# Folded cross attention: folding by pieces, outputs by two batches, norm by four tiles, the last batch by halves

## The chip, the cores and the metric

One core of a Trainium2 chip runs the whole network in one launch. The metric is the device time in microseconds. A core has a matrix engine, TensorE (PE in the profile, its weight loads PEld), a vector engine, VectorE (DVE), a scalar engine, ScalarE (ACT), a general one, GpSimd (POOL), and SyncE (SP), which here only issues transfers. Each runs its own queue of instructions in order. TensorE writes to PSUM, which has eight banks of 128 x 512 float32.

## The reference

Four layers, each a cross attention, a mixer and a mixture of experts, all in float32, over x of 16 batches x 64 tokens x 256. The change is in the cross attention of the second and the third layer (names L1_xattn and L2_xattn), both with this reference, on x after a layer norm without weights, and a context of 1024 tokens x 192 a batch:

```python
def _L2_xattn_ref(x, context, Wq, Wk, Wv, Wo, bo):
    HEADS = 8
    DIM_HEAD = 64
    SCALE = DIM_HEAD ** (-0.5)
    q = (x @ Wq).reshape(B, Nq, HEADS, DIM_HEAD)
    k = (context @ Wk).reshape(B, context.shape[1], HEADS, DIM_HEAD)
    v = (context @ Wv).reshape(B, context.shape[1], HEADS, DIM_HEAD)
    sim = jnp.einsum('bihd,bjhd->bhij', q, k) * SCALE
    attn = jax.nn.softmax(sim, axis=-1)
    out = jnp.einsum('bhij,bjhd->bihd', attn, v)
    return out.reshape(B, Nq, HEADS * DIM_HEAD) @ Wo + bo
...
x = x + _L2_xattn_ref(_layernorm(x, axis=-1), ctx_768, ...)
```

## The kernel before

`xattn_folded` never forms keys or values. It multiplies queries by Wk first ("folding": qw has 192 rows a head, so that scores are qw times the raw context), and applies Wv after the weighted sum of the context. x stands in SBUF as `X`, eight tiles of 128 tokens; `xn` is its norm and `xnT` the transposed norm.

- **Head of a stage.** `norm_T` (line 244) runs the layer norm of all eight tiles: statistics on DVE, the inverse root on POOL (`rsqrt`), the scaling on DVE, eight transposes of four tiles on PE into two banks, two copies; the second four tiles follow. Then `folded(0)`.
- **Folding.** For a group of G = 4 batches (256 tokens), `queries(g, m)` makes the queries of two heads (two matmuls to psq, a scaled copy to qT on ACT) and `fold(g, m)` multiplies them by Wk (four matmuls of 64 rows to two banks psqw, copies by DVE and ACT to qw). `folded` runs all four m in one go; in the main loop it stands ahead of the scores of the group's first batch.
- **Main loop.** A step is half a batch (four heads), 32 steps. In it PE makes the scores of the next step (`scores`: 64 matmuls into four banks pss, with the sums of the last step, psm, between), then the value products of the batch before: `values` (four matmuls of 512 columns on the first 128 context columns) in each half, and `others` (eight, on the other 64) in the second half. Steps with h = 0 are short, those with h = 1 long. DVE finds the maxima (`least`), ACT takes exponentials (`exps`), both scale by the inverse sums (`shares`), DVE transposes (`turn`). `keep` copies a finished batch out of banks o0 and o1 into oc.
- **Outputs.** Every G2 = 4 batches, one batch late, `output` multiplies oc by Wv (16 matmuls pso of 256 columns into two banks), copies them to oT by DVE and ACT, and multiplies two token tiles by Wo (psy), each added to X by DVE.
- **Banks.** `ps_s` has five banks (tag s: scores, psq, psqw, transposes), `ps_t` one (tag t: psm, pso, psy), `ps_o` two (o0, o1).
- **Beside it.** The second cross attention also computes the taps of the next mixer (`conv_taps`, steps 3 to 11: two pieces a step, each POOL, ACT, POOL, DVE in turn); the third takes the context's statistics (`ctx_sigma`, 16 DVE instructions and a root on POOL) in each long step. `add_row` adds the bias row to X on POOL.

After `set_order(True)` the order of PE is that of the code, by `mm` and `tr`, and so is that of DVE and ACT for calls through `dve` and `act` (`in_order` ties each instruction to the one before it on its engine). What is issued through `nc.vector` is placed by the scheduler. Line 188 is `mm`, 191 `tr`, 251 the transposes of `norm_T`, 72 every call through `dve` or `act`.

## Time and profile before

| what | time |
|---|---|
| median of 3 runs (3170.1 to 3172.38) | 3171.4 us |
| the profiled execution | 3170.8 us |
| its span, first to last instruction | 3168.8 us |
| PE busy in the span | 2940.9 us (93%) |
| DVE, ACT, POOL busy | 1960.3, 1348.4, 712.7 us |
| mean granted PE clock | 0.953 |

The second cross attention lies at about 748.7 to 1208.9 us of the span, the third at 1641.0 to 2104.0. In a profile line, "out<-in" are the program's names, "128*32 128x256 f32" the tile of the array and the moving operand, "x64" how many records are merged; a float32 matmul has two records. A bracket tells how long the engine was idle just before and whose end released it. Matmuls are pipelined, so a merged line's duration runs a little past the start of the next.

### The profile page before, as it was taken

What the parts mean: (1) busy time and instruction counts of PE and PEld (TensorE: products, weight loads), DVE (VectorE), ACT (ScalarE), POOL (GpSimd) and SP (SyncE); (2) the same over time, 40 slices, a digit from 0 to 9 for tenths busy, and PEclk for the clock granted to TensorE, in tenths of its full rate; (3) what the DMA queues carried; (4) which work ended last, traced back from release to release, by engine and by line L of the source; (5) the groups of instructions that cost most, each with busy time, mean ns of one, the idle gap of its engine ahead of it and who ended that gap; (6) DMA issues with size and microseconds to landing.
All of it is one profiled execution on the core that took longest, in us unless ns stands there. A gap on an engine that the chain in (4) does not pass through costs nothing.

```text
span 3168.8 us, 64106 instructions
## 1 busy us (share of the span) xinstructions
PE 2940.9 (93%) x26912; PEld 1772.9 (56%) x26912; DVE 1960.3 (62%) x4061; ACT 1348.4 (43%) x3035; POOL 712.7 (22%) x784
## 2 busy tenths in 40 slices
PE   7999999898899999979978999997999899998797
PEld 4666666665445544458854545434665455556676
DVE  6888886524666665971127676757884676765611
ACT  3555554312554541013324454438861255654211
POOL 1000002411110001014411000024771355541131
PEclk9999999999999999978988999998999999999889
DMA  2000000013223313017851222201111211210233
GB/s 74 32 32 32 28 22 15 14 37 105 61 78 92 98 45 82 21 65 270 294 162 53 70 71 73 59 21 39 41 54 37 64 57 63 70 44 14 94 108 122
DMA packets 73793, 223.00 MB, mean 70 GB/s; under 512 B 17457, under 2 KB 28580, under 8 KB 66594
## 3 DMA queue, kind: packets, MB, share of 16 engines
q1 hardware_dynamic: 45936, 113.99, 11.9%
q0 software_dynamic: 21840, 99.39, 9.4%
q10 hardware_dynamic: 5730, 5.53, 0.6%
q8 instruction: 212, 3.47, 0.5%
q14 instruction: 75, 0.61, 0.1%
HBM read 210.00 MB, written 12.66 MB: 70 GB/s over the span
## 4 chain that ended last, share of the span: by engine, by line
PE 79%; DVE 9%; issue 4%; ACT 4%; POOL 3%; DMA 1%; SPq 0%; ACTq 0%; POOLq 0%; DVEq 0%
PE pss L188 13%; PE o L188 12%; PE pu L188 6%; PE psp L188 5%; PE pkv L188 5%; PE pd L188 5%; PE py L188 4%; PE pst L191 4%; PE psc L188 3%; PE po L188 2%; DVE nm L72 2%; ACT pr L72 2%; PE pb L191 2%; PE psi L188 1%; PE psq L188 1%
## 5 line engine op out<-in xcount | busy, mean ns | idle before, releaser
L188 PE MATMUL pss<-cT,qw 128*32 128x256 f32 x8192 | 371.5, 387 | 23.0 <-ACT pr L72 23.0
L72 DVE TENSOR_REDUCE nm<-pss 128x2 f32<-128x512 f32 (+1 forms) x384 | 309.3, 861 | 86.3 <-PE pss L188 86.3
L188 PE MATMUL o<-pT,cx 128*64 128x512 f32 (+1 forms) x1024 | 355.4, 607 | 0.0
L72 ACT ACTIVATE pr<-pss,nmm 128x256 f32<-128x256 f32 x512 | 234.3, 483 | 164.8 <-DVE nmm L72 164.8
L188 PEld LDWEIGHTS pss<-cT,qw 128*32 128x32 f32 x8192 | 205.0, 110 | 173.0 <-ACT pr L72 33.1
L188 PEld LDWEIGHTS o<-pT,cx 128*64 128x64 f32 (+1 forms) x1024 | 127.8, 165 | 200.2 <-issue 187.8
L205 POOL TENSOR_SCALAR rs<-mv 128x8 f32<-128x8 f32 (+3 forms) x52 | 10.0, 193 | 877.1 <-DVE mv L221 444.4
L188 PE MATMUL pkv<-wx,cT 128*128 128x512 f32 (+1 forms) x512 | 193.3, 632 | 0.6 <-issue 0.6
L72 ACT ACTIVATE pr<-pr,sm 128x256 f32<-128x256 f32 x256 | 109.1, 497 | 184.2 <-DVE sm L72 184.2
L72 DVE TENSOR_SCALAR pr<-pr,sm 128x256 f32<-128x256 f32 (+1 forms) x384 | 170.6, 486 | 6.6
L72 DVE TENSOR_TENSOR_SCAN h<-dA,pb 128x512 f32<-128x512 f32 x128 | 154.5, 1217 | 15.8 <-PE pb L191 9.4
L1444 POOL TENSOR_TENSOR h<-h,cb 128x1024 f32<-128x1024 f32 x64 | 151.4, 2368 | 53.3 <-DVE h L72 51.0
L2304 DVE TENSOR_SCALAR y<-pd,row 128x256 f32<-128x256 f32 x39 | 18.9, 484 | 225.1 <-PE pd L188 175.7
L72 DVE STREAM_TRANSPOSE pT<-pr 128x1024 f32<-128x1024 f32 x128 | 151.8, 1224 | 2.2
L188 PE MATMUL pd<-wd,hT 128*128 128x256 f32 x656 | 149.3, 382 | 3.0 <-DVE hT L2492 1.4
L72 ACT ACTIVATE pr<-pss,nm 128x1024 f32<-128x1024 f32 x128 | 142.5, 1113 | 11.4 <-DVE nm L72 8.8
L191 PE MATMUL pst<-ident,pr 128*128 128x128 f32 x1024 | 140.6, 280 | 5.8 <-DVE sm L72 1.9
L72 ACT COPY pT<-pst 128x512 f32<-128x512 f32 x128 | 74.9, 585 | 163.8 <-PE pst L191 163.8
L191 PEld LDWEIGHTS pst<-ident,pr 128*128 128x128 f32 x1024 | 109.4, 141 | 61.5 <-ACT pT L72 26.5
L188 PEld LDWEIGHTS pd<-wd,hT 128*128 128x128 f32 x656 | 123.1, 190 | 31.4 <-DVE hT L2492 6.2
L1618 POOL TENSOR_TENSOR rnk<-rnk,mhalf 128x8 f32<-128x8 f32 (+1 forms) x84 | 130.0, 1548 | 7.0
L188 PE MATMUL py<-h,ident 128*128 128x512 f32 x256 | 130.7, 596 | 0.0
(525 smaller groups left out, 5700.2 us busy)
## 6 DMA issues: line engine op xcount, KB each, us to landing
cT<-in_ctxT SPq DMA_DIRECT2D x32, 768.0 KB, 4.4
cx<-in_ctxP SPq DMA_DIRECT2D x32, 768.0 KB, 4.3
cT<-in_ctxT SPq DMA_DIRECT2D x32, 512.0 KB, 4.3
cT<-in_ctxT SPq DMA_DIRECT2D x64, 256.0 KB, 6.1
offb<-d_off SPq DMA_DIRECT2D x16, 576.0 KB, 3.6
cb<-d_C SPq DMA_DIRECT2D x16, 512.0 KB, 3.8
wu<-in_L_ffn_w POOLq DMA_DIRECT2D x8, 1024.0 KB
wd<-in_L_ffn_w POOLq DMA_DIRECT2D x8, 1024.0 KB
```

The costliest lines, as they stand in the source:

```text
L72: ins = getattr(self.engine, op)(*args, **kwargs)
L188: self.in_order(self.nc.tensor.matmul(out, lhsT=lhsT, rhs=rhs, start=start, stop=stop))
L191: self.in_order(self.nc.tensor.transpose(out, in_, self.ident))
L205: nc.gpsimd.tensor_scalar(t[:p, :n], in_, scale, eps, ALU.mult, ALU.add)
L1444: nc.gpsimd.tensor_tensor(hs[i], hs[i], cbs[hf, g], ALU.mult)
L1618: nc.gpsimd.tensor_tensor(r, r, self.mhalf[:, : n * H], ALU.pow)
L2304: nc.vector.tensor_scalar(y[:, i, :], po[:, i * D : (i + 1) * D], weight[:, g + i : g + i + 1], None, ALU.mult)
```

## The change

Both stages change alike, as they are one function:

- `fold` is split: it makes one pair of heads, into a bank of ps_s and bank o1 (at the start, when nothing else uses them, also into o0 and t), and the new `folded` copies it. From group 1 on, the short steps hold one fold each and the long steps one `queries` each, so that a fold follows its queries by a step. qT is copied by DVE, not ACT. qw is now a tile for four heads, four buffers.
- G2 is 2: `heads` (16 matmuls of 128 columns into one bank t, one copy by ACT) runs in the short step of every second batch, `output` (one token tile) in the long step after it.
- The norm runs by four tiles, its instructions through `dve` and `act`: the first four ahead of the loop, the others in steps 1 (statistics), 2 (scaling) and 3 (transposes). An activation of one element with Exp stands ahead of all.
- Ahead of the loop all four queries of group 0 and the first of group 1 are made, then two folds, the scores of four heads, and then the other two folds.
- In the last step `values` of the batch before stands ahead of the sums; the last batch's products are made for columns 0 to 255 and then 256 to 511, with one `keep` after both.
- `add_row` is called in step 5 instead of step 2.

```diff
--- before.py
+++ after.py
@@ -522,7 +522,7 @@
-        G, G2 = 4, 4
+        G, G2 = 4, 2
         T, T2 = G * TQ, G2 * TQ
         with ExitStack() as es:
             one = es.enter_context(tc.tile_pool(name=f"{L}one", bufs=1))
@@ -534,42 +534,67 @@
 
-            self.norm_T(ps_s, "s")
+
+            stats = one.tile([P, NT, 6], F32, name="stats")
+            mv = one.tile([P, NT, 2], F32, name="mv")
+            rs = one.tile([P, NT], F32, name="rs")
             self.set_order(True)
-            qws, qTs, ctxs, cxs, pTs, outs, ocs = ({} for _ in range(7))
+
+            act.activation(self.small.tile([P, 1], F32, tag="scrap", name="scrap"), self.ones[:, 0:1], AF.Exp)
+            qws, qTs, ctxs, cxs, pTs, outs, ocs, oTs = ({} for _ in range(8))
 
             def bank(name):
                 return ps_s.tile([P, 512], F32, tag="s", name=name)
 
+            def norm(g):
+                ts = slice(4 * g, 4 * g + 4)
+                for t in range(4 * g, 4 * g + 4):
+                    dve.bn_stats(stats[:, t, :], self.X[:, t, :])
+                    dve.bn_aggr(mv[:, t, :], stats[:, t, :])
+                self.rsqrt(rs[:, ts], mv[:, ts, 1], 1.0, 1e-5, 4)
+
+            def normed(g):
+                for t in range(4 * g, 4 * g + 4):
+                    dve.tensor_scalar(
+                        self.xn[:, t, :], self.X[:, t, :], mv[:, t, 0:1], rs[:, t : t + 1], ALU.subtract, ALU.mult
+                    )
+
+            def norm_T(g):
+                for c, copy in enumerate((dve.tensor_copy, act.copy)):
+                    ps = bank("psT")
+                    for k in range(4):
+                        self.tr(ps[:, k * P : (k + 1) * P], self.xn[:, 4 * g + k, c * P : (c + 1) * P])
+                    copy(self.xnT[:, c, g * 512 : (g + 1) * 512], ps)
+
             def queries(g, m):
 
                 tok = slice(g * T, (g + 1) * T)
-                qT = qTs[m] = two.tile([P, T], F32, tag="qT", name="qT")
+                qT = qTs[g, m] = two.tile([P, T], F32, tag="qT", name="qT", bufs=5)
                 ps = bank("psq")
                 for k in range(2):
                     self.mm(ps[:, :T], wq[:, k, m * P : (m + 1) * P], self.xnT[:, k, tok], k == 0, k == 1)
-                act.mul(qT, ps[:, :T], float(DK**-0.5))
-
-            def fold(g, m):
-
-
-                if m == 0:
-                    qws[g] = two.tile([P, 2, G, H, TQ], F32, tag="qw", name="qw", bufs=1)
-                qT = qTs[m]
-                pss = [bank("psqw") for _ in range(2)]
+                dve.tensor_scalar(qT, ps[:, :T], float(DK**-0.5), None, ALU.mult)
+
+            def fold(g, m, other=False):
+
+                if m % 2 == 0:
+                    qws[g, m // 2] = two.tile([P, 2, G, 4, TQ], F32, tag="qw", name="qw", bufs=4)
+                qT = qTs[g, m]
+                if other:
+                    pss = [pool.tile([P, 512], F32, tag=n, name="psqw") for pool, n in ((ps_o, "o0"), (ps_t, "t"))]
+                else:
+                    pss = [bank("psqw"), ps_o.tile([P, 512], F32, tag="o1", name="psqw")]
                 for i in range(2):
                     for hh in range(2):
                         r = slice(hh * DK, (hh + 1) * DK)
                         self.mm(pss[hh][:, i * T : (i + 1) * T], wkT[r, m, i * P : (i + 1) * P], qT[r, :])
-                for hh, copy in enumerate((dve.tensor_copy, act.copy)):
-                    copy(qws[g][:, :, :, 2 * m + hh, :], pss[hh].rearrange("p (i b q) -> p i b q", i=2, q=TQ))
-
-            def folded(g):
-                queries(g, 0)
-                for m in range(4):
-                    if m < 3:
-                        queries(g, m + 1)
-                    fold(g, m)
+                return g, m, pss
+
+            def folded(g, m, pss):
+                for hh, copy in enumerate((act.copy, dve.tensor_copy)):
+                    copy(
+                        qws[g, m // 2][:, :, :, 2 * (m % 2) + hh, :], pss[hh].rearrange("p (i b q) -> p i b q", i=2, q=TQ)
+                    )
 
             def load(b):
 
@@ -592,14 +617,14 @@
                 if h == 0:
                     load(b)
                 c0, c1 = ctxs[b]
-                qw = qws[b // G]
+                qw = qws[b // G, h]
                 pss = [bank("pss") for _ in range(4)]
 
                 def score(k, u, i, rows, start, stop):
                     for qa in range(4):
                         self.mm(
                             pss[k][qa * 32 : (qa + 1) * 32, u * 256 : (u + 1) * 256],
-                            qw[rows, i, b % G, 4 * h + k, u * 32 : (u + 1) * 32],
+                            qw[rows, i, b % G, k, u * 32 : (u + 1) * 32],
                             (c0, c1)[i][rows, :, qa, :],
                             start,
                             stop,
@@ -666,18 +691,22 @@
                     pr.rearrange("p q (k y) -> p q k y", y=32),
                 )
 
-            def values(b, r):
-
-                if r == 0:
-                    outs[b] = [ps_o.tile([P, 512], F32, tag=n, name=n) for n in ("o0", "o1")]
-                for j in range(4 * r, 4 * r + 4):
-                    self.mm(outs[b][0], cxs[b][:, j, 0:P], pTs[b][:, j], j == 0, j == NKC - 1)
-
-            def others(b):
-
+            def values(b, js, cols=slice(0, 512)):
+
+                if js[0] == 0 and cols.start == 0:
+                    outs[b] = [ps_o.tile([P, 512], F32, tag="o0", name="o0"), None]
+                for j in js:
+                    pT = pTs[b][:, j].rearrange("p q x -> p (q x)")
+                    self.mm(outs[b][0][:, cols], cxs[b][:, j, 0:P], pT[:, cols], j == 0, j == NKC - 1)
+
+            def others(b, cols=slice(0, 512)):
+
+                if cols.start == 0:
+                    outs[b][1] = ps_o.tile([P, 512], F32, tag="o1", name="o1")
                 for j in range(NKC):
                     rows = slice((j % 2) * 64, (j % 2 + 1) * 64)
-                    self.mm(outs[b][1][rows, :], cxs[b][:, j, P:C], pTs[b][:, j], j < 2, j >= NKC - 2)
+                    pT = pTs[b][:, j].rearrange("p q x -> p (q x)")
+                    self.mm(outs[b][1][rows, cols], cxs[b][:, j, P:C], pT[:, cols], j < 2, j >= NKC - 2)
 
             def keep(b):
                 if b % G2 == 0:
@@ -686,43 +715,50 @@
                 for i, o in enumerate(outs[b]):
                     (dve.tensor_copy, act.copy)[i](ocs[b // G2][:, i, :, ts], o.rearrange("p (h q) -> p h q", q=TQ))
 
-            def output(g2):
+            def heads(g2):
+
                 oc = ocs[g2]
-                oT = one.tile([P, 4, T2], F32, tag="oT", name="oT")
-                for mp in range(2):
-                    ps = (ps_t, ps_s)[mp].tile([P, 2, T2], F32, tag="ts"[mp], name="pso")
-                    for mi in range(2):
-                        for i in range(2):
-                            for hh in range(2):
-                                h = 4 * mp + 2 * mi + hh
-                                self.mm(
-                                    ps[hh * DK : (hh + 1) * DK, mi, :],
-                                    wv[:, i, h * DK : (h + 1) * DK],
-                                    oc[:, i, h, :],
-                                    i == 0,
-                                    i == 1,
-                                )
-                    (dve.tensor_copy, act.copy)[mp](oT[:, 2 * mp : 2 * mp + 2, :], ps)
-                for tt in range(T2 // P):
-                    t = g2 * T2 // P + tt
-                    ps = ps_t.tile([P, 512], F32, tag="t", name="psy")
-                    for m in range(4):
-                        self.mm(ps[:, :D], oT[:, m, tt * P : (tt + 1) * P], wo[:, m, :], m == 0, m == 3)
-                    dve.tensor_tensor(self.X[:, t, :], self.X[:, t, :], ps[:, :D], ALU.add)
-
-            folded(0)
+                oT = oTs[0] = one.tile([P, 4, T2], F32, tag="oT", name="oT")
+                ps = ps_t.tile([P, 4, T2], F32, tag="t", name="pso")
+                for m in range(4):
+                    for i in range(2):
+                        for hh in range(2):
+                            h = 2 * m + hh
+                            self.mm(
+                                ps[hh * DK : (hh + 1) * DK, m, :], wv[:, i, h * DK : (h + 1) * DK], oc[:, i, h, :], i == 0, i == 1
+                            )
+                act.copy(oT, ps)
+
+            def output(t):
+                ps = ps_t.tile([P, 512], F32, tag="t", name="psy")
+                for m in range(4):
+                    self.mm(ps[:, :D], oTs[0][:, m, :], wo[:, m, :], m == 0, m == 3)
+                dve.tensor_tensor(self.X[:, t, :], self.X[:, t, :], ps[:, :D], ALU.add)
+
+            norm(0)
+            normed(0)
+            norm_T(0)
+            for m in range(4):
+                queries(0, m)
+            queries(1, 0)
+            for m in range(2):
+                folded(*fold(0, m, m == 1))
             steps = [(b, h) for b in range(B) for h in range(2)]
             pss = scores(0, 0, None)
-            now = exps(pss, least(pss))
+            pieces = [fold(0, m, m == 3) for m in (2, 3)]
+            m = least(pss)
+            for x in pieces:
+                folded(*x)
+            now = exps(pss, m)
             st = {}
             for i, (b, h) in enumerate(steps):
                 ahead = steps[i + 1] if i + 1 < len(steps) else None
-                if ahead and ahead[0] % G == 0 and ahead[1] == 0:
-                    folded(ahead[0] // G)
+                g, at = (i + 1) // 8, (i + 1) % 8
                 prs, sm = now
                 if ahead:
                     pss = scores(*ahead, lambda: sums(st, sm))
                 else:
+                    values(b - 1, range(4, NKC))
                     sums(st, sm)
                 dve.reciprocal(sm, st["sum"][:, :8])
                 shares(prs, sm, 1)
@@ -731,17 +767,31 @@
                 shares(prs, sm, 0)
                 turn(b, 2 * h, prs[0])
                 turn(b, 2 * h + 1, prs[1])
-                if b > 0:
-                    values(b - 1, h)
-                    if h == 1:
-                        others(b - 1)
-                        keep(b - 1)
+                if ahead and b > 0:
+                    values(b - 1, range(4 * h, 4 * h + 4))
+                if b > 0 and h == 1:
+                    others(b - 1)
+                    keep(b - 1)
+                if i == 1:
+                    norm(1)
+                if i == 2:
+                    normed(1)
+                if i == 3:
+                    norm_T(1)
+
+                if h == 0 and g + 1 < B // G:
+                    folded(*fold(g + 1, at // 2))
+                if h == 1 and (i + 2) // 8 + 1 < B // G and i + 1 < 2 * B:
+                    queries((i + 2) // 8 + 1, (i + 2) % 8 // 2)
                 if h == 1 and L == "L2_xattn":
                     self.ctx_sigma(b, cxs[b], dve)
-                if b == 1 and h == 0:
+                if i == 5:
                     self.add_row(f"{L}_bo", one)
-                if h == 0 and b % G2 == 1 and b > 1:
-                    output(b // G2 - 1)
+                if b % G2 == 1 and b > 1:
+                    if h == 0:
+                        heads(b // G2 - 1)
+                    else:
+                        output(b // G2 - 1)
                 if L == "L1_xattn":
 
                     if i == 3:
@@ -752,11 +802,12 @@
                     if 14 <= i < 14 + TQ // 4:
                         for t in range(4):
                             self.tap_rows(4 * (i - 14) + t)
-            for r in range(2):
-                values(B - 1, r)
-            others(B - 1)
+            for cols in (slice(0, 256), slice(256, 512)):
+                values(B - 1, range(NKC), cols)
+                others(B - 1, cols)
             keep(B - 1)
-            output(B // G2 - 1)
+            heads(B // G2 - 1)
+            output(NT - 1)
             self.set_order(False)
 
 
```

## The prediction

> **What bounds the kernel now.** The busy line of the page comes first: TensorE (PE) 93%, VectorE (DVE) 62%, ScalarE (ACT) 43%. That is an average over twelve stages, so I cut the two stages that change into a head, a steady stretch and a tail, by windows (columns: window, its length, busy us and count of PE, weight loads, DVE, ACT, POOL, granted PE clock, DMA share, GB/s). First the second cross attention, then the third:
> ```profile
> 748.70:808.40 59.70, 44.55 (x609) 25.61 (x608) 31.06 (x81) 23.34 (x74) 8.78 (x16) 0.86 0.40 113
> 808.40:1171.36 362.96, 351.24 (x4538) 182.59 (x4537) 230.33 (x543) 178.81 (x618) 24.20 (x37) 0.99 0.28 79
> 1171.36:1208.90 37.54, 32.30 (x128) 14.33 (x120) 14.49 (x33) 7.50 (x24) 2.21 (x4) 0.91 0.23 52
> ...
> 1641.00:1705.40 64.40, 45.84 (x624) 26.00 (x624) 38.03 (x102) 23.66 (x76) 10.12 (x16) 0.81 0.34 91
> 1705.40:2063.70 358.30, 351.77 (x4521) 182.37 (x4521) 266.47 (x726) 172.41 (x597) 27.34 (x31) 0.99 0.23 68
> 2063.70:2104.00 40.30, 35.44 (x148) 16.34 (x141) 23.36 (x69) 8.65 (x26) 8.27 (x14) 0.96 0.06 14
> ```
> Both stages are bound by PE. Their PE stands idle for about 32 and 30 us, and the granted clock below 1 costs some more. That is all a reordering can win here. PE's own timeline shows where it lies. The folding of a group of four batches, then an output block, then the tail:
> ```profile
> 964.51 1.89 PE L188 MATMUL psq<-xnT,wq 128*128 128x256 f32 x8
> 968.04 1.13 PE L188 MATMUL psqw<-qT,wkT 64*128 64x256 f32 x8 [1.64 <-ACT qT L72]
> ...
> 974.22 3.66 PE L188 MATMUL pss<-cT,qw 128*32 128x256 f32 x64
> ...
> 1123.18 3.67 PE L188 MATMUL pso<-oc,wv 128*64 128x256 f32 x32
> ...
> 1129.29 1.99 PE L188 MATMUL psy<-wo,oT 128*128 128x256 f32 x8 [0.51 <-DVE X L72]
> 1131.22 3.66 PE L188 MATMUL pss<-cT,qw 128*32 128x256 f32 x64
> ...
> 1171.36 3.70 PE L188 MATMUL o<-pT,cx 128*128 128x512 f32 x8
> 1178.15 0.30 PE L188 MATMUL psm<-sm,same 128*32 128x8 f32 x8 [3.10 <-ACT pr L72]
> ...
> 1199.85 3.24 PE L188 MATMUL pso<-oc,wv 128*64 128x256 f32 x28 [0.25 <-ACT oc L72]
> ...
> 1208.91 1.75 PE L251 MATMUL psT<-ident,xn 128*128 128x128 f32 x14 [1.38 <-DVE X L72]
> ```
> A fold block holds PE from 964.51 to 974.22, 9.71 us, and inside it PE waits for ACT, which still has exponentials ahead of qT. The first steps of a stage, before value products exist, are bound by latency:
> ```profile
> 777.64 4.48 PE L188 MATMUL pss<-cT,qw 128*32 128x256 f32 x48 [4.28 <-ACT pr L72]
> ...
> 788.05 1.41 PE L188 MATMUL pss<-cT,qw 128*32 128x256 f32 x12 [3.00 <-ACT pr L72]
> ```
> PE waits there until exponentials free score banks, and the 48 matmuls after the wait take 4.48 us against 2.6 (48 x 54 ns, from 3.48 us for 64 in the steady part): they run on half the clock.
>
> **The change, part by part.**
>
> *Folding by pieces (both stages).* The fold blocks before last 15.57, 9.71, 9.71 us in the second cross attention (the first one waits 4.57 us because qT stands behind the tap exponentials on ACT) and 9.71, 11.35, 9.72 in the third; sums 35.0 and 30.8. After, each becomes four folds of 1.06 us (the start to start of 8 psqw records) and four queries of 0.97 (4 records x 216 ns plus 0.1 for the switch). They sit behind values and others, whose inputs are ready, and qT is made a step earlier, so no wait remains. Of the twelve of each, two folds and two queries fall into the first steps; ten of each cost 10.6 + 9.7 = 20.3. Gain 14.7 and 10.5 us.
>
> Its price is hidden in the banks. A step takes four score banks of five; before, the fifth let the next step start while the exponentials still held the others. Now each piece takes the fifth, so the next scores need the first freed bank. In the steady third stage the first two exponentials end 9.6 us after a step's scores start; PE arrives after 5.5 + 3.63 + 1.06 = 10.2 us. So 0.6 us of cover is left in short steps and over 3 in long ones: cost nothing, and every us beyond 0.6 would count fully. Queued behind the new DVE qT are ctx_sigma (3.84 us) and the next reciprocal: qT ends 0.55 us into the next step, sigma at 4.4, the reciprocal at 4.7, and the maxima that need it out of the way start at 4.9. Cover 0.2, cost nothing. In the tap steps of the second stage two taps add 4.2 us to the chain of ACT and DVE (11.5 us a step, 12.05 with the folded copy: 23.6 a pair); PE's pair is now 23.8, or 27.4 with outputs. Again hidden.
>
> *Outputs by two batches.* Before 9.41 + 8.04 + 8.04 = 25.5 and 24.1 us for three blocks. After, six heads and six outputs in this stretch (the seventh goes to the tail), with ACT's copy between them a step away. An output is 8 x 216 ns + 0.2 = 1.93. A head has 32 records of 128 columns, which the trace does not show. At 256 columns 32 records took 3.6 us (1123.18 to 1126.79), half of that is 1.93 with the switch kept; the nearest small row, 64 columns in the same 128 x 64 tiling, has 72 records in 2.32 us, 31 ns each, so nothing holds a record above its 54 ns. The Trainium skill speaks against it: "TensorE: Matmul & The Clock Gate", Back-to-back issue gap, gives about 81 ns a matmul at 128 columns sustained with weight loads. By it a head is 2.8 us, and 16 heads cost 14 us more; I take the row. 12 x 1.93 = 23.2. Gain 2.3 and 0.9. PSUM's one "t" bank is free in time: the oT copy ends some 13 us into a step of 12, the next sums need it at 15.5.
>
> *Norm by four tiles.* PE's path to the first score loses the second half of norm and its transposes, and four of the eight pieces: in the third stage psT ends at 1646.7 as before, then five queries (20 records, 4.3 us warm, up to 6.7 while cold) and two folds (2.1) put the first score at 1654.3 to 1655.9 against 1659.23. In the second stage the statistics now stand behind the last X update on DVE instead of between updates, so psT ends near 756.0 and scores start at 763.5 to 765.1 against 766.8. Gain 2.5 and 4 us (middles). The other 16 transposes cost 16 x 109 ns + 0.2 = 1.9 us in step 3, and norm(1) 2.3 and 1.4 us of DVE in steps 1 and 2. The early exponential meant to load ACT's table does not do so: in the changed program's order both such activations stand at the program's start and a table load still stands right ahead of the first real one. Its 1.28 us (ACT at 775.27) stay; the Trainium skill, "ScalarE: Activation LUTs", What ACT_TABLE_LOAD costs, would put a switch at 2.66 with its drain, but Exp started at 776.56, so no drain is seen and the sum would differ by nothing, as nothing moves.
>
> *The first steps get worse.* With the fifth bank taken, a step redoes all four score groups after the exponentials instead of three: 0.87 us in each of three or four steps. From first score to the scores of batch 2: before 41.6 us (766.8 to 808.4), after 10.8 to the second step's scores, 11.3 each to the third's and fourth's (3.5 scores, 1.7 cold loss, 6.1 to the freed bank), then 5.2 + 2.05 + 3.45 + 1.06 through the second fold: 45.2. Loss 3.6; in the third stage, where before took 45.3 and norm(1) now delays the maxima by some 1.9, loss 1.8. A cold window more or less is 1.7 us.
>
> *The tail.* Before, from the end of the last scores: 1171.36 to psT at 1208.91, 37.5 us, with 3.1 of wait, half a clock for 6.8 us, and pso, copies and psy of four batches in a row. After: values 3.45, heads 1.93, values 3.45 (in the wait's place), sums 0.2, others 3.5, psy 1.93, the last batch 10.7, then 5.4 for oc copy, heads, oT copy, psy: 30.6. Gain 7.0. The third stage ends on X's last tile through norm to psi (3.6 us behind X): 5.5. Halving the last batch wins nothing of it, as keep still follows both halves.
>
> *Sum.* Second: 14.7 + 2.3 - 1.9 + 2.5 - 3.6 + 7.0 = 21.0. Third: 10.5 + 0.9 - 1.9 + 4.0 - 1.8 + 5.5 = 17.2. The profiled span of 3168.8 falls by 38.2 to 3130.6; what lies around the span and the medians put the measured time 2.6 above it (3171.4), so 3133.
>
> **The rivals.** *Pieces, but smaller gain*: switches of tiling (0.1 us at some 33 places a stage, 6.6 in all), heads by the rule (14), a cold window more in each start. Each alone leaves 3136 to 3147. For it: psq between psqw costs 1.06 where 0.87 is its work. *The waits stay*: qT or folded copies still come late behind ACT and DVE queues, so the folding gain (25.2) goes and head and tail remain: 3158. Against: a whole step lies between query and fold. *Slower*: the fifth bank. If the first freed bank comes later than 0.6 us after PE's arrival in short and long steps alike, each of 48 pieces pays; it turns the sign when PE waits 0.8 us at each (38.2 / 48), and at 1.2 the time is 3191. It would need exponentials 1.4 us later than measured. *The norm and tail alone fail* (starts cold, next stage not waiting for X): minus 19, 3152.
>
> **How the numbers follow.** Forecast as summed 0.70, smaller gain 0.14, waits stay or head and tail fail 0.09, slower 0.05, nothing visible (gains eaten one by one) 0.02. The range takes 3122 (cold windows kinder by three in each stage) to 3150 (switches and 81 ns heads partly true). 0.2%, 6 us, is what a measurement tells from no change: faster 0.93, same 0.02, slower 0.05.
>
> **What would show it.** No wait for qT ahead of psqw; heads of 32 records near 1.9 us; no wait of 3 us ahead of the last psm; first scores 2 to 4 us sooner after X; PE idle in the steady stretches below 4 us. Waits "<-ACT pr" ahead of pss in steps with a fold would make the prediction wrong, as would heads near 2.8 us.

## The result

The changed kernel takes 3139.3 us, the kernel before 3171.9 us in the same trial: a ratio of 0.988, 95% interval 0.984 to 0.993. The forecast was 3133. The profiled execution took 3139.8 us with a span of 3138.1, 30.7 us below that of before. (The granted clock, a column of the windows, is the share of its full clock that PE was given.) Its windows over the same three stretches of each stage, with the columns of the prediction's first table:

```profile
746.70:806.02 59.32, 45.96 (x629) 27.05 (x627) 36.10 (x95) 22.79 (x74) 6.20 (x11) 0.86 0.44 118
806.02:1152.98 346.96, 346.96 (x4618) 182.92 (x4616) 232.15 (x552) 174.10 (x605) 27.25 (x41) 1.00 0.28 83
1152.98:1184.44 31.46, 29.74 (x192) 18.60 (x184) 13.72 (x31) 7.99 (x25) 1.89 (x4) 1.00 0.15 33
...
1627.40:1685.82 58.42, 42.83 (x625) 25.49 (x625) 38.20 (x110) 22.17 (x72) 4.29 (x6) 0.88 0.39 100
1685.82:2036.09 350.27, 350.15 (x4616) 183.33 (x4616) 269.96 (x734) 168.59 (x588) 32.63 (x38) 0.99 0.24 70
2036.09:2070.90 34.81, 32.45 (x208) 20.46 (x200) 21.84 (x67) 8.58 (x26) 7.13 (x12) 1.00 0.07 16
```

In the steady stretches PE is busy for 346.96 of 346.96 us and 350.15 of 350.27, so no idle time is left to win there. PE's timeline of the second cross attention, a short step with its fold and heads, then the tail:

```profile
850.17 3.70 PE L188 MATMUL o<-pT,cx 128*128 128x512 f32 x8
853.80 1.14 PE L188 MATMUL psqw<-qT,wkT 64*128 64x256 f32 x8
854.86 1.97 PE L188 MATMUL pso<-oc,wv 128*64 128x128 f32 x32
856.76 3.66 PE L188 MATMUL pss<-cT,qw 128*32 128x256 f32 x64
...
1152.98 3.70 PE L188 MATMUL o<-pT,cx 128*128 128x512 f32 x8
1156.62 1.97 PE L188 MATMUL pso<-oc,wv 128*64 128x128 f32 x32
1158.51 3.70 PE L188 MATMUL o<-pT,cx 128*128 128x512 f32 x8
1162.14 0.25 PE L188 MATMUL psm<-sm,same 128*32 128x8 f32 x8
...
1179.44 1.75 PE L188 MATMUL pso<-oc,wv 128*64 128x128 f32 x28 [0.47 <-ACT oc L72]
1181.93 1.99 PE L188 MATMUL psy<-wo,oT 128*128 128x256 f32 x8 [0.74 <-ACT oT L72]
1184.44 1.75 PE L251 MATMUL psT<-ident,xn 128*128 128x128 f32 x14 [0.51 <-DVE X L72]
```

A fold takes 1.06 us from start to start (853.80 to 854.86) and waits for nothing. A head of 32 records takes 1.90 us (854.86 to 856.76), 59 ns a record. No bracket stands before the sums at 1162.14.

The terms, in us (a minus is a loss), from the start of the last X update to the first psi of the mixer behind:

| | second, forecast | second, measured | third, forecast | third, measured |
|---|---|---|---|---|
| X to first score | 2.5 | 2.7 | 4.0 | 4.6 |
| first score to scores of batch 2 | -3.6 | -2.3 | -1.8 | 1.6 |
| steady stretch | 15.1 | 16.0 | 9.5 | 8.8 |
| end of last scores to the next stage | 7.0 | 6.1 | 5.5 | 4.2 |
| sum | 21.0 | 22.5 | 17.2 | 19.3 |

In the third stage of before a quarter of the scores of batch 2 ran ahead at 1701.90 and the rest followed at 1705.43; its boundary is set 0.87 us ahead of the rest, as in the prediction's 45.3. With the window's 1705.40 instead, the second and third row of that column read 2.5 and 8.0.

The two stages gave 41.7 us where 38.2 were forecast. Yet the span fell by only 30.7. The gap opens outside the change, in the mixer after the second cross attention (12.2 us lost; elsewhere 1.2 were won), where a dense gate projection (psi, 2 records of 512 columns) and 32 small Toeplitz matmuls (psT, 64 x 64 with 8 columns) take turns. Its windows in the profiled execution of each, of before (the whole stretch, then its end) and of after:

```profile
1337.41:1376.54 39.13, 39.13 (x543) 24.35 (x542) 38.66 (x62) 6.62 (x11) 0.71 (x1) 0.81 0.04 15
1361.41:1376.54 15.13, 15.13 (x140) 8.95 (x136) 14.66 (x33) 1.75 (x3) 0.71 (x1) 0.51 0.02 4
```

```profile
1313.56:1364.89 51.33, 51.33 (x543) 31.31 (x542) 38.64 (x62) 6.62 (x11) 0.71 (x1) 0.59 0.03 10
1322.94:1364.89 41.95, 41.95 (x378) 25.07 (x374) 29.26 (x52) 4.87 (x8) 0.71 (x1) 0.50 0.00 1
```

The same 543 records, PE busy throughout in both by the profile, no waits, and 12.2 us more: the granted clock halves 24 us into the stretch in before and 9 us into it in after. Both then keep the half clock to the end. A pair of turns, psi and psT, takes:

```profile
1320.85 1.12 PE L188 MATMUL psi<-xnT,w_in 128*128 128x512 f32 x2
1321.91 1.10 PE L188 MATMUL psT<-xt,T 64*64 64x8 f32 x32
1322.94 2.01 PE L188 MATMUL psi<-xnT,w_in 128*128 128x512 f32 x2
1324.88 1.88 PE L188 MATMUL psT<-xt,T 64*64 64x8 f32 x32
```

That is 2.09 us at the full clock, 3.75 in the first pair at half (start to start), 3.81 in later ones.

### The profile page after: what moved, and what is told of

It is laid out like the page before. It is cut to its first block, busy times and chain, and to the rows that moved or that the text cites. A ratio compares the mean times of both kernels' runs of the same rounds, so it can differ in the third digit from the quotient of the medians.

```text
span 3138.1 us, 64791 instructions
## 1 busy us (share of the span) xinstructions
PE 2942.0 (94%) x27232; PEld 1792.9 (57%) x27232; DVE 1966.8 (63%) x4085; ACT 1340.0 (43%) x3013; POOL 712.7 (23%) x780
## 4 chain that ended last, share of the span: by engine, by line
PE 81%; DVE 7%; issue 5%; POOL 2%; ACT 2%; DMA 2%; SPq 0%; POOLq 0%; ACTq 0%; DVEq 0%
PE pss L188 15%; PE o L188 13%; PE psp L188 5%; PE pu L188 5%; PE pkv L188 5%; PE pd L188 5%; PE py L188 4%; PE pst L191 4%; PE psc L188 3%; PE po L188 2%; PE pb L191 2%; PE psq L188 2%; PE psi L188 1%; PE psy L188 1%; PE pg L188 1%
## 5 line engine op out<-in xcount | busy, mean ns | idle before, releaser
L188 PE MATMUL o<-pT,cx 128*64 128x512 f32 (+3 forms) x1088 | 351.7, 576 | 0.0
L188 PEld LDWEIGHTS o<-pT,cx 128*64 128x64 f32 (+1 forms) x1088 | 134.2, 163 | 188.4 <-issue 161.8
L188 PEld LDWEIGHTS pkv<-wx,cT 128*128 128x128 f32 (+1 forms) x512 | 64.5, 189 | 118.4 <-issue 92.2
```

The lines of the kernel that those rows point to most:

```text
L188: self.in_order(self.nc.tensor.matmul(out, lhsT=lhsT, rhs=rhs, start=start, stop=stop))
```

## The experiments

Times of whole runs turned out to carry the clock of every other stage. Four runs of one kernel (the eighth below) took 3124.5, 3132.0, 3134.0 and 3144.2 us at mean clocks of 0.961, 0.959, 0.958 and 0.955. So each edit is read from its stages, whose lengths in two profiles with the same instructions mostly agree within 0.1 us, or within one to three us where the clock in a stage's head differs. All stage lengths run from the start of the last X update before the stage to the first psi after it. The medians come from several trials, in which that of before itself lay between 3171.9 and 3190.5:

| kernel | second | third | sum | median |
|---|---|---|---|---|
| before | 461.1 | 459.8 | 920.9 | 3171.9 |
| after | 438.6 | 440.6 | 879.2 | 3139.3 |
| 3: before, dense mixer | 461.2 | 456.5 | 917.7 | 3176.7 |
| 4: after, dense mixer (the base) | 438.4 | 439.2 | 877.6 | 3125.0 |
| 5: folds whole | 444.3 | 444.8 | 889.1 | 3144.7 |
| 6: last batch whole | 438.0 | 440.6 | 878.6 | 3130.2 |
| 7: norm whole | 439.1 | 439.9 | 879.0 | 3135.4 |
| 8: sums first | 440.1 | 440.1 | 880.2 | 3133.0 |
| 9: tuned | 436.4 | 436.2 | 872.5 | 3117.7 |
| 10: copies on ACT | 438.4 | 441.8 | 880.2 | 3135.4 |
| 11: exponentials held | 438.4 | 464.6 | 903.1 | 3156.1 |
| 12: outputs alone | 450.9 | 449.0 | 900.0 | 3152.1 |

**The mixer's clock: a finer mix (1 and 2).** In the records of the granted clock of all fourteen traces, every half-clock stretch lasts a whole multiple of 3.41 us (but the last of each, which the end of the program cuts). First theory: pairs of turns of 2.09 us beat against that period, so finer turns would hold the clock up.

```diff
-                toeplitz(i, (n for h in range(2) for n in project(4 + i, h)))
+                toeplitz(i, (n for h in range(2) for n in project(4 + i, h, 2)))
...
-                    if d % (TB // 4) == 0:
+                    if d % (TB // 8) == 0:
```

> The kernel before, with one thing changed in the mixer behind each cross attention: the gate projection beside the Toeplitz products is cut into two pieces of 256 columns, so that dense (psi) and sparse (psT) work of TensorE alternate every 1.03 us instead of every 2.07 us; the matmul work is the same. Theory (the loss of 12.8 us behind the second stage is TensorE's clock, dropping on the alternation): the half clock that before shows from 1361.7 to 1382.1 is gone, about 4 pairs of 3.81 instead of 2.07 us, minus 7: 3164 to 3165. Rival (the loss is a lasting effect of the changed stage on its follower, the alternation has no part in it): 3171, the same within 0.2%.

> The changed kernel with the same finer alternation in the mixer. Theory (clock): the half clock from 1323 to 1371 is gone, some 11 pairs at 3.81 instead of 2.07 us, minus 19: 3120 to 3121, and between this and the kernel before with the same edit lie the gains of the two stages alone, 41 to 44 us. Rival (lasting effect of the stage): no lower than 3135, and 28 to 32 us below its counterpart.

The kernel before came to 3187.2 us (ratio 1.004, 1.002 to 1.005), beyond both expectations; the changed one to 3147.1, where the rival had it, though 40.1 below its counterpart, near the theory's 41 to 44. The window of the stretch in the first of them (this profile is of the slowest of its ten runs, 3198.8 us):

```profile
1338.26:1402.01 63.75, 63.75 (x574) 43.52 (x574) 38.90 (x62) 6.62 (x11) 0.66 (x1) 0.53 0.02 8
```

Now the half clock begins some 3 us into the stretch (24 in before) and lasts to its end; the stretch takes 63.75 us. In the changed kernel with this edit it begins after 9 us, as without it, and the stretch took 59.3. So the time does hang on the clock in this stretch, as the theory said, but finer turns do not hold the clock up: it falls sooner in one kernel and no later in the other.

**The mixer's clock: a denser mix (3 and 4).** The next theory was that the share of dense work decides, and that more work should cost less.

```diff
+                    for s in range(2):
+                        half = slice(n * 512 + s * 256, n * 512 + (s + 1) * 256)
+                        for k, last in ((0, True), (0, False), (1, True)):
+                            self.mm(
+                                ps[:, s * 256 : (s + 1) * 256],
+                                w_in[:, k, c * P : (c + 1) * P],
+                                self.xnT[:, k, half],
+                                k == 0,
+                                last,
+                            )
+                        if s == 0:
+                            yield
```

> The kernel before, with MORE work in the mixer's alternating stretch: each half of a gate projection makes its first matmul of 256 columns twice (the second one starts the sum afresh, so the values are unchanged). The dense block between two sparse ones grows from 1.05 to about 1.57 us, and its share of the time from one half to six tenths. New theory (TensorE's clock goes by the share of dense work in each 3.41 us window, and the even mix lies at the edge, so that one low window starts a half clock that keeps itself up): the 16 pairs stay warm at 2.6 us each, 41.6 us, against 12 x 2.07 + 4 x 3.81 = 40.1 before: plus 1.5, 3173. Rival (the half clock comes from what ran earlier, whatever the mix): half of the pairs cold at 4.8 us, 59 us: plus 19, 3190.

> The changed kernel with the same extra work. New theory (share of dense work): 41.6 us warm against 5 x 2.07 + 11 x 3.81 = 52.3 in the changed kernel: minus 10.7 in spite of 16 x 0.52 us more work, 3128 to 3129; and 42 to 45 us below the kernel before with the same edit, which is the gain of the two stages alone. Rival (history): 11 pairs at 4.8 and 5 at 2.6 us, 66 us: plus 14, 3153.

Measured: 3176.7 us (ratio 1.001, 0.999 to 1.003) and 3125.0 (0.985, 0.983 to 0.987). The stretch of the second:

```profile
1316.11:1355.08 38.97, 38.97 (x603) 32.03 (x602) 38.20 (x61) 6.61 (x11) 0.71 (x1) 1.00 0.04 13
```

60 records more than in after, and 12.4 us less; the theory had 41.6 us, the rival 66. In the profiles of all ten kernels with this mix (3 to 12) the stretch lasts 38.96 or 38.97 us at the full clock, whatever ran before it. So what ran before does not lower the clock by itself; the mix must allow it. What makes the half clock of one and the same mix begin after 24 us in before and 9 us in after, and so what links the change to the 12.2 us, is not shown: what ran before and chance are both open. The edit takes the clock of this stretch out of the comparison: the stages of 3 and 4 differ by 40.1 us. Their medians differ by more, 51.8; the rest lies in other stages, at mean clocks of 0.953 and 0.961. Three mixes do not separate the share of dense work (at the full clock 0.51, 0.53 and 0.59 of the time) from the length of a dense turn; both grew in the last one. That stays open.

**Folding by pieces undone (5), outputs by two alone (12).**

```diff
+                if ahead and at == 0:
+                    queries(g, 0)
+                    for m in range(4):
+                        if m < 3:
+                            queries(g, m + 1)
+                        folded(*fold(g, m))
...
-                if h == 0 and g + 1 < B // G:
-                    folded(*fold(g + 1, at // 2))
-                if h == 1 and (i + 2) // 8 + 1 < B // G and i + 1 < 2 * B:
-                    queries((i + 2) // 8 + 1, (i + 2) % 8 // 2)
```

> From here on the base is the changed kernel with the denser mixer stretch (3125.0 us), whose times scatter least; it is named the base below. Here the folding by pieces alone is undone in it: groups 1 to 3 are folded in one block ahead of their first scores, qT on ACT, both banks of the five. Theory (the pieces bring 14.7 and 10.5 us in the steady stretches, and cost 2 to 4 in all in the first steps): plus 21 to 23, 3146 to 3148, with waits for qT ahead of psqw back. Rival (the waits of the blocks were the norm's and outputs' doing, the pieces bring only their bank's trouble): plus 5 or less, 3130.

The stages grew by 11.5 us only, half of what was expected. (The median rose by 19.8; 12.5 of the spans' difference lie behind the third stage's end.) What went missing shows in the waits of psqw, here of before and of this kernel:

```profile
L188 PE MATMUL psqw<-qT,wkT x256: 376/376/792, 760.4 to 1971.4; 64*128 64x256 f32 x128
its engine sat idle before it (us, times) until:
  ACT qT L72: 12.8, 6
```

```profile
L188 PE MATMUL psqw<-qT,wkT x256: 376/376/792, 760.5 to 1944.7; 64*128 64x256 f32 x128
its engine sat idle before it (us, times) until:
  ACT qT L72: 6.6, 2
```

Whole blocks are back, but only the first of each stage waits for ACT. So something else in the change had taken the other four waits away. The theory: outputs by two put heads, 1.9 us of PE work, into the short step right ahead of each block, and ACT uses that time to finish its exponentials. The twelfth run tests it from the other side: the kernel before (with the dense mixer), G2 = 2, `heads` in the short step and `output` in the long one, and nothing else of the change.

```diff
-        G, G2 = 4, 4
+        G, G2 = 4, 2
...
-                if h == 0 and b % G2 == 1 and b > 1:
-                    output(b // G2 - 1)
+                if b % G2 == 1 and b > 1:
+                    if h == 0:
+                        heads(b // G2 - 1)
+                    else:
+                        output(b // G2 - 1)
```

> The kernel before with the denser mixer stretch (3176.7 us) and of the change only the outputs by two batches (heads in the short step, output in the long one). Additive theory (the terms of the prediction stand alone): 3.2 in the steady stretches and about 6 in the tails, minus 9 to 10 in the two stages together, the waits of 1.65 us for qT in the fold blocks stay. Other theory (the output moved into the long step ahead of each group gives ACT time, so that the waits in the fold blocks, some 6 to 7 us, go with it, and the heads fill half of the tail's 3.1 us): minus 17 to 20 in the two stages.

The stages fell by 10.2 and 7.5, together 17.7 us, against run 3, where the additive theory had 9 to 10 and the other 17 to 20. A fold block with the heads ahead of it, and the tail:

```profile
966.76 1.97 PE L188 MATMUL pso<-oc,wv 128*64 128x128 f32 x32
968.66 1.99 PE L188 MATMUL psq<-xnT,wq 128*128 128x256 f32 x8
970.69 1.13 PE L188 MATMUL psqw<-qT,wkT 64*128 64x256 f32 x8
971.75 1.13 PE L188 MATMUL psq<-xnT,wq 128*128 128x256 f32 x4
...
1177.19 0.25 PE L188 MATMUL psm<-sm,same 128*32 128x8 f32 x8 [1.68 <-ACT oT L72]
```

No wait stands ahead of psqw, neither in this block nor in the four others that had waited 1.65 us in before; one of the six, of 4.3 us, is left. The last exponential of the step ends 3.06 us after the block's start in before (964.51 to 967.57) and 1.07 us after it here (968.66 to 969.73). The block takes 8.2 us (968.66 to 976.87, the next scores) instead of 9.7. The trace shows how the two parts share the gain, by the time from a stage's first scores to those of batch 4, where the second group begins, and from there to the last scores:

| kernel | second, to batch 4 | second, on | third, to batch 4 | third, on |
|---|---|---|---|---|
| before | 100.8 | 303.4 | 100.5 | 303.7 |
| 3: before, dense mixer | 100.9 | 303.4 | 99.3 | 302.0 |
| 12: outputs alone | 102.7 | 296.2 | 100.9 | 296.2 |
| 5: folds whole | 101.1 | 296.1 | 102.7 | 296.1 |
| 4: base | 92.9 | 295.9 | 96.6 | 296.2 |

From batch 4 on, outputs by two alone bring 7.2 and 5.9 us against run 3, nearly the whole gain there, and pieces add 0.3 at most: four folds and four queries cost PE as much in a block as apart once nothing waits. (The 1.6 us that before has beyond run 3 in the third stage are a half clock in its block of 11.35 us. Up to batch 4 run 12 takes 1.8 and 1.6 us more than run 3, as its first heads fall there.) The pieces' gain stands ahead of batch 4, 8.1 and 6.1 us from the first scores; 5.9 and 5.6 are left in the stage lengths, as the first scores come 2.5 and 0.4 us later with the pieces and their early query. Ahead of batch 4 the pieces remove the first block's wait (4.26 and 2.36 us in 5) and the half clock behind it:

```profile
855.00 2.08 PE L188 MATMUL psqw<-qT,wkT 64*128 64x256 f32 x8 [4.26 <-ACT qT L72]
857.01 2.08 PE L188 MATMUL psq<-xnT,wq 128*128 128x256 f32 x4
```

The clock of 5 is 0.50 from 853.1 to 859.9 us; these two lines usually take 1.13 us each. The first blocks of 5 last 14.74 and 12.40 us instead of 8.21, which is 6.5 and 4.2 us of the gain; the rest is not taken apart. Pieces without outputs by two were not tried, so whether the pieces alone would remove the four other waits is not shown.

**The tail (6 and 8).** All columns at once, and the sums ahead of the values again:

```diff
-            for cols in (slice(0, 256), slice(256, 512)):
+            for cols in (slice(0, 512),):
```

> The base with the last batch's products made for all 512 columns at once instead of two halves. Theory (halving wins nothing, keep stands behind both): no difference over 0.5 us a stage, 3125. Rival (the halves shorten the tail): plus 2 to 4, 3127 to 3129.

```diff
-                    values(b - 1, range(4, NKC))
                     sums(st, sm)
...
-                if ahead and b > 0:
+                if b > 0:
                     values(b - 1, range(4 * h, 4 * h + 4))
```

> The base with the last step's sums ahead of the values of the batch before, as in the kernel before. Theory (the values fill the wait of 3.1 us for the last exponentials): that wait is back in both stages, plus 6, 3131, and nearly all of the tail's gain besides is from the outputs by two. Rival (the last batch's own chain sets the tail's end anyway): plus 1 or less, 3125 to 3126.

Whole, the last batch is quicker: the tails (last score to first psi) are 0.40 and 0.31 us shorter, 32 long records taking 10.6 us and 64 short ones 11.0. The 1.4 us more in the third stage of 6 arose in its head and first steps, where the clock was halved for 19.6 us against 14.8 in the base. With the sums first the tails grew by 1.7 and 0.7 us, not by 3.1 each. The line of 8:

```profile
1155.32 1.97 PE L188 MATMUL pso<-oc,wv 128*64 128x128 f32 x32
1158.96 0.25 PE L188 MATMUL psm<-sm,same 128*32 128x8 f32 x8 [1.67 <-ACT oT L72]
```

The heads already stand where PE waited 3.10 us in before, so there is a wait of only 1.67 left to fill; it ends with the copy of oT, which gives the sums their bank back and stands behind the last exponentials on ACT. In the third stage one of 0.47 for oc then stands where the base has 1.56.

**The norm (7).** Both calls ahead of the loop, none in steps 1 to 3.

```diff
-            norm(0)
-            normed(0)
-            norm_T(0)
+            for g in range(2):
+                norm(g)
+            for g in range(2):
+                normed(g)
+                norm_T(g)
```

> The base with the norm of all eight tiles ahead of the loop. Theory: the first score comes later by the second four tiles' statistics and transposes, 3 to 4 us a stage, and step 3 is rid of 1.9 us of transposes: plus 2 to 4 in all, 3127 to 3129. Rival (the norm inside the first steps holds up the maxima and costs what it wins): 3121 to 3125.

X to first score grew by 2.9 and 3.1 us, the loop shrank by 2.3 and 2.4: the norm by four wins 0.7 us a stage. The signs are the theory's, the sum (1.4) lies between it and the rival. Of the 9.9 us between the spans of this kernel and the base, 8.5 lie outside the two stages.

**The fifth bank (9, 10 and 11).** The tuned kernel gives the bank back in the first two steps and keeps the last batch by halves:

```diff
+                elif early:
+                    pss = [ps_o.tile([P, 512], F32, tag=n, name="psqw") for n in ("o0", "o1")]
...
-                    folded(*fold(g + 1, at // 2))
+                    folded(*fold(g + 1, at // 2, early=i == 0))
...
+                ps = ps_o.tile([P, 512], F32, tag="o0", name="psq") if early else bank("psq")
...
+            for hs in (slice(0, 4), slice(4, 8)):
+                cols = slice(hs.start * TQ, hs.stop * TQ)
+                values(B - 1, range(NKC), cols)
+                others(B - 1, cols)
+                keep(B - 1, hs)
```

> The base with two small mends: in the first two steps, where o0 and o1 hold nothing yet, the fold and the query use them and leave the fifth score bank alone; and the last batch's results are kept by halves, the first half's copies beside the second half's products. Theory: one score group less to redo in one or two steps of each stage (0.9 us each) and 0.2 to 0.3 us less wait for the last oc: minus 2 to 4 in all, 3121 to 3123. Rival (the first steps wait for the exponentials whichever bank is free): minus 0.5, 3124 to 3125.

3117.7 us, 0.978 of before (0.974 to 0.982), which ran at 3190.5 in that trial; the stages are 2.1 and 3.0 us shorter than the base's, more than the 2 to 4 in all that were expected, of that 0.7 and 1.1 in the tails. The third scores of the second stage, in the base and then here:

```profile
784.82 5.35 PE L188 MATMUL pss<-cT,qw 128*32 128x256 f32 x64 [2.94 <-ACT pr L72]
```

```profile
781.61 1.07 PE L188 MATMUL pss<-cT,qw 128*32 128x256 f32 x16
784.62 4.48 PE L188 MATMUL pss<-cT,qw 128*32 128x256 f32 x48 [1.94 <-ACT pr L72]
```

With a spare bank a quarter of the scores runs ahead of the wait, and 48 records instead of 64 come after it: 0.87 us, the price that the prediction gave. In the steady part, the claim was that 0.6 us of cover is left. A first attempt put two copies ahead of the exponentials:

```diff
+                if L == "L2_xattn":
+                    for c in range(2):
+                        act.copy(idle, self.xnT[:, c, :])
```

> The price of the fifth bank: the base with two copies of 1024 columns (about 2 us) put ahead of each step's exponentials on ACT in the third cross attention only; they write to a tile that nobody reads. Theory (0.6 to 0.7 us of cover in short steps without heads, 2.6 in those with heads, over 4 in long ones): waits of about 1.4 us for the exponentials ahead of pss in the 7 or 8 short steps without heads, none elsewhere, plus 10 in that stage, 3135. Rival 1 (a spare bank is free in time, the cover is larger): no waits, 3125. Rival 2 (the chain of ACT and DVE becomes the bound): every step 2 us longer, plus 50 to 60, 3180.

It told nothing of the steady part: ACT had been idle for 2.70 us there, waiting for the maxima, and the copies (2.10 us) ran in that time. The exponentials began 8.51 us after their scores' start, as in the base, and from batch 4 to the last scores both took 296.16 us. Made to wait for the maxima, they do their work:

```diff
-                        act.copy(idle, self.xnT[:, c, :])
+                        act.mul(idle, self.xnT[:, c, :], m[:, 0:1])
```

> The base again with two operations of 1024 columns on ACT ahead of each step's exponentials in the third cross attention, now multiplied by the maxima, so that they can't start before these and do hold up the exponentials by 2.1 us (the copies of the last trial ran in 2.7 us in which ACT was waiting anyway, and moved nothing). Theory (fifth bank; 0.7 us of cover in short steps without heads, 2.6 in those with heads, 4 in long ones): waits of 1.4 us ahead of pss in the 7 short steps without heads, plus 10, and some 2 us more in each of the 3 latency-bound first steps, plus 6: plus 15 to 16 in that stage. Rival (the cover is larger): nothing in the steady steps, plus 6 in the first ones. Rival (the chain of ACT and DVE becomes the bound): plus 50 to 60.

```profile
1816.02 3.70 PE L188 MATMUL o<-pT,cx 128*128 128x512 f32 x8
1819.65 1.14 PE L188 MATMUL psqw<-qT,wkT 64*128 64x256 f32 x8
1822.25 3.80 PE L188 MATMUL pss<-cT,qw 128*32 128x256 f32 x64 [1.46 <-ACT pr L72]
```

The third stage grew by 25.5 us: 9.3 up to the scores of batch 2 (6 expected), 16.2 after (10 expected). In the steady part a short step with a fold and no heads takes 11.74 us instead of 10.21, and the long step behind it 13.94 instead of 13.80; those with heads stay at 12.11, but for the first. The exponentials begin 10.69 us after their scores' start instead of 8.52. So 2.17 us of delay less the 1.53 by which the short step grew leaves 0.64 us of cover, as forecast. The theory had missed two things. The first step with heads and the long one behind it pay 3.6 us together; its exponentials are 2.7 us late in the base too. And the last batches have no pieces: there PE arrives a fold earlier, so a pair of steps pays 1.9 us in spite of its spare bank.

## Why the prediction was right, and where not

- **Folding by pieces and outputs.** The steady stretches gained 24.8 us, 24.6 were forecast. The split between the two terms was wrong. In the groups behind the first, blocks of 9.71, 9.71 and 11.35, 9.72 us were to shrink by the pieces, and outputs to bring 2.3 and 0.9. There the outputs alone bring 7.2 and 5.9 us, the waits for qT among them, and with them in place the pieces win only in the first group. That "no wait remains" was right, but for all blocks behind the first of each stage the outputs suffice. So the sum of the two terms came out by luck, the work of one set down to the other.
- **Heads.** 1.90 us each where 1.93 was taken from the row of 256 columns. The 81 ns a matmul of the Trainium skill ("TensorE: Matmul & The Clock Gate", Back-to-back issue gap) would have made about 2.6 of it (an estimate, 32 x 81 ns; the prediction said 2.8); here a record of 128 columns took 59.
- **The fifth bank.** "0.6 us of cover": 0.64 by the held exponentials. The rival on the slower side has its mechanism shown, but needs exponentials later than they are, and then mainly short steps pay, not all 48 pieces.
- **Head of the stage.** 2.7 and 4.6 for 2.5 and 4. The norm's part in it is some 3 us a stage, paid back by 2.3 in the loop.
- **First steps.** "Loss 3.6" and "loss 1.8" came out as a loss of 2.3 and a gain of 1.6. The step that failed is "a step redoes all four score groups after the exponentials instead of three", taken for "each of three or four steps". In the first of them 16 records still ran ahead of the wait. In the third stage the granted clock over the head and the first steps was 0.88 against 0.81 besides. Nor did the table load stay where it was: it ran at 770.24 us, 0.28 us before the maxima were ready. The 0.87 us for such a step was right.
- **Tail.** 6.1 and 4.2 for 7.0 and 5.5. The mis-sized term is the end behind the last batch's products: 5.4 was taken, and 5.9 passed in the second stage (1178.59 to 1184.44); in the third the last heads waited 1.57 us for oc. Values "in the wait's place" is true, but heads take 1.4 of its 3.1 us first. "Halving the last batch wins nothing of it": it costs 0.3 to 0.4.
- **The sum.** The stages gave 41.7, the median 32.6. The step that failed is the silent one, that everything outside the two stages stays as it was ("The profiled span of 3168.8 falls by 38.2"). One mixer took 12.2 us back by its clock, and the edit that steadies that clock gave 12.4 back. A rule of the same page of the Trainium skill speaks here: against drops of throughput in mid-kernel it asks for no PE-idle gaps over some 3 us between matmuls ("TensorE: Matmul & The Clock Gate", Why this matters for your kernels). If that were enough, the stretch would stay at 2.09 us a pair, 33 us for its 16 pairs. The row says 51.33 us with PE busy in all of them and a clock of 0.59, so for this mix the rule is not enough. Why the clock fell sooner there than in before stays open. The range (3122 to 3150) held the time by its width, not because it had named this cause.

## What to carry to other kernels

A part of a change can remove a wait that was put down to another part, as the outputs did here; sum what is won per wait and not per edit, and expect a part undone alone to return less than its share. When a stage gets shorter, look at the granted clock of the stages behind it, and compare kernels by the lengths of the stages that differ. A long stretch that alternates dense matmuls with small ones can lose nearly half its speed with the engine never idle (3.81 us a pair instead of 2.09). In this one stretch more dense work made the time lower, so that is worth a try.

## What the hardware showed

A PE that is busy in every microsecond was throttled to half its clock (51.33 us busy of 51.33, clock 0.59), and in all four profiles without the denser mix (before, after, 1 and 2) it stayed there from its first half-clock turn to the end of the stretch. With 0.59 of the time dense instead of 0.51 it never happened in ten profiles. 603 records then took 38.97 us where 543 had taken 51.33.
